# Weights through GpSimd's queue in the load stage, a comparison in two parts, and the last X W products between own half rows

## The chip, the cores and the metric

The kernel runs on one core of one Trainium2 chip. The metric is the device time of one execution in microseconds (us). Three timed executions of the kernel before gave 1069.7, 1071.4 and 1076.45 us, with the median 1071.4 us.

## The reference, cut to what matters

Four graph layers with a residual and a layer norm behind each work on N = 2708 nodes with 128 features and a 2708 x 2708 adjacency matrix in float32.

```
x = norm(x + L0(x, adj));  x = norm(x + L1(x, adj));  x = norm(x + L2(x, adj));  x = norm(x + L3(x, adj))

L0: d = 1/sqrt(adj.sum(-1));  z = leaky_relu((d * (adj @ (d * x))) @ W1 + b1, 0.1)
    S = exp(-dist(z_i, z_j) / 2), only the 4 largest of a row kept
    A2 = S + adj;  d2 = 1/sqrt(A2.sum(-1));  out = (d2 * (A2 @ (d2 * x))) @ W2 + b2
L1: XW = X @ W;  c = XW @ a[:128];  r = XW @ a[128:]
    den = exp(leaky_relu(r[:, None] + c[None, :], 0.01));  num = A @ den
    att = where(num != 0, den / num, 0);  H = A @ (att @ XW)
L2: d = 1/sqrt(adj.sum(1) + 1e-6);  (d * (adj @ (d * x))) @ W.T + b
L3: relu(concat([x, adj @ x]) @ W.T + b)
```

In L1 the kernel sorts the nodes by c, so that the two branches of the leaky relu become sums over the nodes on either side of an edge in that order. For this it needs the rank of every node's c among all c.

## The kernel before, in words

The matrix is passed in transposed. It is cut into 22 row tiles of 128 rows (the last one has 20) and into six column chunks with 512, 512, 512, 512, 384 and 276 columns. Row tiles 0 to 15 are streamed in panels of four tiles; tiles 16 to 21 stay in the resident tile `res`, filled chunk by chunk.

**Load stage** (lines 461 to 520). A loop over the chunks c = 0 to 5 issues, all on SyncE's queue (SP): the rows of x (`load_x`, L132), three panels into a pool of four `part` buffers and the fourth panel into a slot of `ring` (`load_panel`, L178), the resident tiles (L472) and the last 20 rows (L477). VectorE adds all panels into `both` (L479, L483, L484), which gives the degrees of the chunk's nodes; TensorE sums `both` over the partitions (L496); VectorE and ScalarE make `dinv` and the scaled rows `y` of this chunk (L501, L242, L243, L260). TensorE also adds the products of the panels with the y that is known already (`add_group`, L428): in step c the groups g = 0 to c - 1, with the group of chunk c - 1's own panel put in after the first. At c = 4 the eleven loads of weights and biases (`load_const` and `load_rows`, L143) stand behind chunk 4's panels on SP's queue and ahead of chunk 5's. The biases and the attention vector are read as one row repeated for 128 partitions. `ring` and `res` are zeroed first by GpSimd (L125, L120), and a panel that goes into `ring` waits for that. In this stage only TensorE's order is written out by hand; the order of the other engines is a planner's. Behind the loop TensorE adds what is left (`rest`, `add_few`), and the next stage computes all distances for the four nearest neighbours.

**Pass 2 of L0** (`by_panels` with `end_pass2`, L993). Here the order of TensorE, VectorE and ScalarE is the program's. `by_panels` calls a tick after every product, and `end_pass2` places the work on a finished chunk at ticks counted from n: `norm0` (L800, L805), `turn` (transposes L818, copied by ScalarE L821), `find_c` (a product L872 gives the chunk's c for all partitions, copied into `c_row` by ScalarE L873; VectorE L877 takes each node's own c), then for each tile t `compare` (VectorE: a mask of c_row >= c_t, L904, and ties, L914), `times_w` (X W, L885, L886), `rank_rows` (ScalarE sums the mask's rows, L922) and `rank_columns` (TensorE sums its columns, L927). The last chunk (tiles 19 to 21) is done otherwise: `last_stats`, `last_rc` (c and r of the three tiles, L847, L850), `turn_c` (transposes L866, copied into `c_row` by ScalarE L867), then the comparisons of tiles 19 and 20 and `compare_few`. In `find_ranks` (L949) everything is joined.

**Lists of L1** (lines 1104 to 1505). A table `turns` writes out the order: `line` adds one half row tile of the matrix that was streamed into a berth (L1387, 8 matmul records, and the load of the line that follows in this berth, L1062), `own_line` one from `res`, and between them stand the steps that build the sorted lists. `last_xw` forms X W for tiles 19 to 21: a transpose (L1180), ScalarE's copy (L1182), the product (L1184), ScalarE's copy (L1186) and GpSimd's store (L1187), tile after tile. `in_rank_order` and `in_list_order` (L1228) put values into order by one-hot matrices `hot_in` (L1218), `counts` (L1314, L1321) counts list lengths, `ranked` and `listed` write down the indices with which GpSimd gathers rows.

The block stage of L1 and the layers 2 and 3 come behind that. Their text is not touched.

Of the kernel before, what the change touches and what calls it, by code (L numbers as in the profile page):

```python
# [8 lines left out]
F32 = mybir.dt.float32  # L9
U32 = mybir.dt.uint32  # L10
I32 = mybir.dt.int32
BF16 = mybir.dt.bfloat16
# [4 lines left out]
P = 128  # L17
CW = 512
RES = 6
# [33 lines left out]
def kernel(  # L53
# [42 lines left out]
    def few(c):  # L96
        g = c % GROUPS * 32
        return slice(g, g + LAST)
# [41 lines left out]

    def load_const(src, cols, name):
        t = const.tile([P, cols], F32, tag=name, name=name)
        nc.sync.dma_start(t, src)  # L143
        return t

    def load_rows(src, cols, name):
# [217 lines left out]
    with tc.tile_pool(name="knn", bufs=1) as knn:  # L364
# [97 lines left out]
        with (  # L462
# [5 lines left out]
            for c in range(C):  # L468
                w = cw[c]
                load_x(chunk_tiles[c])  # L470
                parts = [load_panel(g, c, load if g < G - 1 else None) for g in range(G)]
                nc.sync.dma_start(  # L472
                    res[:, : FULL - S, cols[c]],
                    adjT[S * P : FULL * P, cols[c]].rearrange("(t p) k -> p t k", p=P),
                )
                if LAST:
                    nc.sync.dma_start(res[few(c), FULL - S, cols[c]], adjT[FULL * P :, cols[c]])  # L477
                both = degp.tile([P, 2, CW], F32, tag="both", name="both")
                nc.vector.tensor_add(both[:, :, :w], parts[0][:, :2, :w], parts[0][:, 2:, :w])  # L479
                more = [part[:, n : n + 2, :w] for part in parts[1:] for n in (0, 2)]  # L480
                more += [res[:, n : n + 2, cols[c]] for n in range(0, RES, 2)]
                for m in more:
                    nc.vector.tensor_add(both[:, :, :w], both[:, :, :w], m)  # L483
                nc.vector.tensor_add(both[:, 0, :w], both[:, 0, :w], both[:, 1, :w])  # L484

                for g in range(min(c, G)):
                    add_group(c, g, parts[g])
                    if wait is not None:
                        add_group(*wait)
                        wait = None  # L490
                if c == C - 1:
                    add_group(c, G, None)
                ts = chunk_tiles[c]
                dps = mis_tile()
                for k, t in enumerate(ts):
                    nc.tensor.matmul(  # L496
                        dps[: pw[t], k : k + 1], lhsT=both[:, 0, k * P : k * P + pw[t]], rhs=ones, start=True, stop=True
                    )
                full = sum(pw[t] == P for t in ts)
                t0, t1 = ts[0], ts[-1] + 1  # L500
                nc.vector.tensor_copy(deg[:, t0 : t0 + full], dps[:, :full])  # L501
                if t0 + full < t1:
                    nc.vector.tensor_copy(deg[:LAST, t0 + full : t1], dps[:LAST, full : full + 1])
                inv_sqrt(dinv[:, t0:t1], deg[:, t0:t1])
                scale_rows(y, xs, dinv, ts)
                if c == C - 1:
                    spread(y[:, FULL, :])
                wait = (c, c, parts[c] if c < G else None, c == C - 1)
                if c == C - 2:
                    w1_sb = load_const(w1, D, "w1")  # L510
                    w2_sb = load_const(w2, D, "w2")
                    wa_sb = load_const(w_att, D, "w_att")
                    wl_sb = load_const(w_lap_t, D, "w_lap")
                    wx_sb = load_const(w_cat_t[:D, :], D, "w_cat_x")
                    wh_sb = load_const(w_cat_t[D:, :], D, "w_cat_h")
                    b1_sb = load_rows(b1, D, "b1")
                    b2_sb = load_rows(b2, D, "b2")
                    bl_sb = load_rows(b_lap, D, "b_lap")
                    bc_sb = load_rows(b_cat, D, "b_cat")
                    a_sb = load_rows(a_att, 2 * D, "a_att")  # L520


            def rest(c, g, end=False):
# [316 lines left out]
            nc.vector.bn_aggr(mv[: pw[t], t, :], st[: pw[t]])  # L840
        inv_sqrt_of(rstd_l, mv[:, l0:l1, 1], LN_EPS, True)

    def last_rc():

        both = rc_of(C - 1, lambda t: P)
        for v, dst in ((1, cc), (0, rr)):
            nc.vector.scalar_tensor_tensor(  # L847
                dst[:, l0:l1], mv[:, l0:l1, 0], w_sum[:, v : v + 1], both[:, v, :], op0=ALU.mult, op1=ALU.subtract
            )
            nc.vector.scalar_tensor_tensor(  # L850
                dst[:, l0:l1], dst[:, l0:l1], -1.0, rstd_l, op0=ALU.mult, op1=ALU.mult
            )

    def last_norm():
        for t in last_ts:
# [40 lines left out]

    split = {T - 2: (T - 1) * P // 2}

    def compare(t):
        p, o = pw[t], t * P  # L900
        s = cc[:p, t : t + 1]
        mask = masks[t] = sum_pool.tile([P, N], BF16, tag="mask", name="mask", bufs=4)
        m = split.get(t, o + p)
        nc.vector.tensor_scalar(mask[:p, :m], c_row[:p, :m], s, None, op0=ALU.is_ge)  # L904
# [84 lines left out]

    ended = [-16]  # L990
    behind_last = []

    def end_pass2(c, acc):  # L993
        n = max(due.n + 1, near_at[chunk_tiles[c][-1]] + 3, ended[-1] + 16)
# [8 lines left out]
        if c < C - 1:  # L1003
            at(n + 2, norm0, ts)
            at(n + 9, turn, c)
            at(n + 11, find_c, c)
            for k, t in enumerate(ts):
                at(n + 13 + 2 * k, compare, t)
                at(n + 14 + 2 * k, times_w, c, t)
# [94 lines left out]
    with tc.tile_pool(name="rank", bufs=1) as rank:  # L1104
# [67 lines left out]
        c_part = pick_c(edge, "first")  # L1172
        last_norm()

        def last_xw():

            for t in last_ts:
                p = pw[t]
                pt = mis_tile()
                nc.tensor.transpose(pt[:, :p], xs[:p, t, :], ident[:p, :p])  # L1180
                xT = small.tile([P, P], F32, tag="z", name="xT")
                nc.scalar.copy(xT[:, :p], pt[:, :p])  # L1182
                po = mis_tile()
                nc.tensor.matmul(po[:p, :D], lhsT=xT[:, :p], rhs=wa_sb, start=True, stop=True)  # L1184
                row = small.tile([P, P], F32, tag="junk", name="row")
                nc.scalar.copy(row[:p], po[:p, :D])  # L1186
                nc.gpsimd.dma_start(xw_rows[t * P : t * P + p, :], row[:p])  # L1187

        def whole(dst, src, n):

# [283 lines left out]
        def own_line(n):  # L1474
# [373 lines left out]
```

## Time and profile before

| | us |
|---|---|
| median of three timed executions | 1071.4 |
| profiled execution, its own time | 1068.27 |
| its span in the profile | 1066.5 |
| load stage, until the last degree sum of TensorE | 0 to 105.6 |
| rest of the first pass and the neighbour search | 105.6 to 300 |
| pass 2 until the last mask product (L942) | 300 to 448.4 |
| lists of L1 | 448.4 to 507 |
| block stage of L1 | 507 to 731 |
| last tiles of L1, layers 2 and 3 | 731 to 1066.5 |

The profile shows one execution. PE is TensorE's matmul, PEld its weight load, DVE VectorE, ACT ScalarE, POOL GpSimd, SP SyncE; SPq is SP's queue. In a timeline a row gives the start, the time taken, the engine, the line, the operation, the tiles (out<-in), the shape, the count and, in brackets, the idle time before it with what ended it. In a table of windows each row is a stretch: its length, then for PE, PEld, DVE, ACT and POOL the busy time and the number of instructions, then the clock granted to TensorE as a share of full speed, the DMA engines' busy share and GB/s.

### The profile page before, as it was taken

How to read it: one execution, taken by the hardware profiler on the slowest of the kernel's cores; microseconds unless marked ns; L12 is line 12 of the kernel's file. 1: busy time of each engine (PE TensorE's matmuls, PEld its weight loads, DVE VectorE, ACT ScalarE, POOL GpSimd, SP SyncE). 2: the span in 40 equal slices, each digit the busy share in tenths (PEclk: the TensorE clock that was granted, in tenths of full speed). 3: DMA queues.
4: the chain of work that ended last, by engine and by line, in shares of the span. 5: the costliest groups of instructions: out<-in, count | busy, mean ns of one | idle time of the engine just before them, and what ended most of it. 6: DMA issues, size and time to landing. Idle time of an engine off the chain costs nothing.

```text
span 1066.5 us, 11660 instructions
## 1 busy us (share of the span) xinstructions
PE 983.9 (92%) x3773; PEld 481.8 (45%) x3773; DVE 637.6 (60%) x1363; ACT 331.9 (31%) x609; POOL 264.9 (25%) x339
## 2 busy tenths in 40 slices
PE   0888999999994998799899999999999999999996
PEld 0346544444442556654333333334445544564444
DVE  5985438999943578674798999995121121222222
ACT  0000126555500244612776776663010100010000
POOL 4000000000564565005766443430121100000000
PEclk9989999999997999699999999999999999999998
DMA  9998350000183666587565455456755856484652
GB/s 338 363 340 268 114 160 1 0 1 1 42 278 113 202 184 209 199 357 260 144 172 150 137 141 165 133 169 202 232 189 173 292 181 216 145 276 145 229 166 74
DMA packets 102001, 191.00 MB, mean 179 GB/s; under 512 B 14022, under 2 KB 43342, under 8 KB 101930
## 3 DMA queue, kind: packets, MB, share of 16 engines
q1 hardware_dynamic: 83896, 152.34, 43.1%
q0 software_dynamic: 17728, 37.62, 12.8%
q8 instruction: 32, 0.52, 0.2%
q14 instruction: 39, 0.32, 0.1%
q10 hardware_dynamic: 306, 0.20, 0.1%
HBM read 214.80 MB, written 4.16 MB: 205 GB/s over the span
## 4 chain that ended last, share of the span: by engine, by line
PE 48%; DVE 1%; ACT 1%; issue 0%; DMA 0%; POOL 0%; SPq 0%; POOLq 0%
PE acc L204 27%; PE hacc L1536 10%; PE num L1654 9%; PE mis L285 1%; PE mis L1783 0%; DMA ring<-carry 0%; ACT gb L234 0%; PE mis L1749 0%; DVE inv L1525 0%; PE mis L1779 0%; DVE inv L1528 0%; ACT inv L1511 0%; POOL rstd L253 0%; DVE err L1521 0%; PE mis L1737 0%
## 5 line engine op out<-in xcount | busy, mean ns | idle before, releaser
L1095 POOL DMA_INDIRECT ring<-in_adjT,slot_i x88 | 96.6, 1098 | 93.8 <-PE num L1654 72.1
L1654 PE MATMUL num<-ring,lw 128*64 128x512 f32 (+1 forms) x528 | 111.9, 550 | 4.0 <-DVE err L1521 1.9
L1536 PE MATMUL hacc<-inv,xws 128*128 128x512 f32 (+1 forms) x264 | 111.7, 559 | 1.7 <-ACT xws L1699 1.4
L705 PE MATMUL acc<-zT,z 128*128 128x512 f32 (+2 forms) x252 | 102.2, 552 | 0.0
L1511 ACT ACTIVATE inv<-num,plain 128x1024 f32<-128x1024 f32 x88 | 80.5, 915 | 59.3 <-PE num L1654 38.9
L253 POOL TENSOR_TENSOR rstd<-rstd,minus_half 128x4 f32<-128x4 f32 (+1 forms) x18 | 17.3, 959 | 313.5 <-DVE rstd L252 313.5
L234 ACT COPY gb<-acc 128x512 f32<-128x512 f32 (+2 forms) x18 | 9.6, 534 | 251.1 <-PE acc L204 251.1
L706 ACT COPY key<-acc 128x512 f32<-128x512 f32 (+2 forms) x126 | 67.1, 534 | 55.1 <-PE acc L705 27.7
L204 PE MATMUL acc<-ring,y 128*128 128x512 f32 (+2 forms) x192 | 83.3, 564 | 0.5 <-issue 0.5
L750 POOL DMA_INDIRECT got<-y_rows,where x66 | 70.8, 1073 | 45.8 <-DVE near_sum L763 25.9
L1536 PEld LDWEIGHTS hacc<-inv,xws 128*128 128x128 f32 x264 | 46.5, 189 | 78.7 <-issue 53.4
L1521 DVE TENSOR_TENSOR err<-inv,num 128x1024 f32<-128x1024 f32 x88 | 73.8, 852 | 10.2 <-DMA carry<-m_rows 4.9
L204 PE MATMUL acc<-ring,xs 128*128 128x512 f32 (+2 forms) x192 | 77.6, 547 | 0.0
L1528 DVE SCALAR_TENSOR_TENSOR inv<-gb,g_inv,inv 128x1024 f32<-128x1024 f32 x88 | 77.0, 912 | 0.1
L204 PE MATMUL acc<-ring,carry 128*128 128x512 f32 (+2 forms) x192 | 74.5, 542 | 0.0
L204 PE MATMUL acc<-ring,m_rows 128*128 128x512 f32 (+2 forms) x192 | 74.3, 542 | 0.0
L1525 DVE SCALAR_TENSOR_TENSOR inv<-err,inv 128x1024 f32<-128x1024 f32 x88 | 72.2, 858 | 0.1
L705 PEld LDWEIGHTS acc<-zT,z 128*128 128x128 f32 x252 | 45.8, 190 | 50.4 <-issue 45.0
L1514 ACT ACTIVATE inv<-inv 128x1024 f32<-128x1024 f32 x88 | 67.6, 768 | 2.8
L575 POOL TENSOR_TENSOR slot_e<-near,sim 128x44 f32<-128x44 f32 (+2 forms) x3 | 0.7, 238 | 259.3 <-DVE near L572 259.2
L709 DVE MAX8 near<-key 128x8 f32<-128x2708 f32 x21 | 62.3, 2965 | 2.6 <-ACT key L706 2.6
L1654 PEld LDWEIGHTS num<-ring,lw 128*64 128x64 f32 x528 | 35.6, 136 | 62.4 <-issue 44.6
(378 smaller groups left out, 1368.9 us busy)
## 6 DMA issues: line engine op xcount, KB each, us to landing
ring<-in_adjT SPq DMA_DIRECT2D x74, 1024.0 KB
ring<-in_adjT SPq DMA_DIRECT2D x20, 677.0 KB
ring<-in_adjT SPq DMA_DIRECT2D x17, 768.0 KB
part<-in_adjT SPq DMA_DIRECT2D x12, 1024.0 KB
ring<-in_adjT SPq DMA_DIRECT2D x17, 552.0 KB
more<-in_adjT SPq DMA_DIRECT2D x10, 677.0 KB
res<-in_adjT SPq DMA_DIRECT2D x4, 1280.0 KB
part<-in_adjT SPq DMA_DIRECT2D x3, 768.0 KB
```

What stands on the lines that cost most here:

```text
L204: nc.tensor.matmul(accs[c][: lhsT.shape[-1], :w], lhsT=lhsT, rhs=src, start=start, stop=stop)
L705: nc.tensor.matmul(pks[c][:p, : cw[c]], lhsT=z2[:, :p], rhs=zT[:, cs], start=False, stop=True)
L706: nc.scalar.copy(key[:p, cs], pks[c][:p, : cw[c]])
L750: nc.gpsimd.indirect_dma_start(out=got[:p, :], out_offset=None, in_=y2_rows[:, :], in_offset=bass.IndirectOffsetOnAxis(ap=where[:p, t, k : ...
L1095: nc.gpsimd.indirect_dma_start(out=rows[i][:KC, n, :], out_offset=None, in_=adj_half[:, :], in_offset=bass.IndirectOffsetOnAxis(ap=slot_i[ ...
L1511: nc.scalar.activation(inv, num[:, :w], AF.Ln, scale=plain[:, 0:1], bias=plain[:, 1:2])
L1514: nc.scalar.activation(inv, inv, AF.Exp, scale=-1.0)
L1521: nc.vector.tensor_mul(err, inv, num[:, :w])
L1525: nc.vector.scalar_tensor_tensor(inv, err, 2.0, inv, op0=ALU.subtract, op1=ALU.mult)
L1528: nc.vector.scalar_tensor_tensor(inv, gb[:, col : col + w], g_inv[:, q : q + 1], inv, op0=ALU.max, op1=ALU.mult)
L1536: nc.tensor.matmul(haccs[:, o:e], lhsT=xws[:, q, :], rhs=inv[:, o:e], start=(q == 0), stop=(q == NQ - 1))
L1654: nc.tensor.matmul(num[n * (BJ + 2) : (n + 1) * (BJ + 2), o:e], lhsT=lw[:, 2 * q + n, :], rhs=rows[i][:, n, c0 + o : c0 + e], start=True, ...
```

## The change

There are five edits.

1. `load_const` issues on GpSimd's queue instead of SP's, and the eleven weight loads stand at c = 1, ahead of that chunk's panels in the program, instead of at the end of c = 4.
2. In chunk 0 the panel that goes into `ring` is issued behind the resident tiles and the last rows, and VectorE adds it last. Chunks 1 to 5 keep their order.
3. The row sum of the mask of tile 15 (the last tile of the fourth chunk) moves on ScalarE behind `turn` and `find_c` of the fifth chunk: `behind_turn`.
4. In the last chunk `last_rc` is split: c of the three tiles comes first, then `turn_c`, then the part of tile 19's mask that needs the columns below 2432 only (`compare_known`), then the rest of it in `compare`; r of the three tiles and its negative come two ticks later, ahead of tile 20's comparison.
5. `last_xw` is split into `turn_last` and `last_xw(t)`, and one line or own half row stands between the two for each of the tiles 19, 20 and 21. Two own lines are taken for that from the group of four ahead of `ranks_known`.

```
     def load_const(src, cols, name):
         t = const.tile([P, cols], F32, tag=name, name=name)
-        nc.sync.dma_start(t, src)
+        nc.gpsimd.dma_start(t, src)
...
                 load_x(chunk_tiles[c])
-                parts = [load_panel(g, c, load if g < G - 1 else None) for g in range(G)]
+                if c == 1:
+                    w1_sb = load_const(w1, D, "w1")
...
+                    a_sb = load_rows(a_att, 2 * D, "a_att")
+                parts = [load_panel(g, c, load) for g in range(G - 1)]
+                if c:
+                    parts.append(load_panel(G - 1, c))
                 nc.sync.dma_start(
                     res[:, : FULL - S, cols[c]],
...
                     nc.sync.dma_start(res[few(c), FULL - S, cols[c]], adjT[FULL * P :, cols[c]])
+                if not c:
+                    parts.append(load_panel(G - 1, c))
...
-                more += [res[:, n : n + 2, cols[c]] for n in range(0, RES, 2)]
+                held = [res[:, n : n + 2, cols[c]] for n in range(0, RES, 2)]
+                more = more + held if c else more[:-2] + held + more[-2:]
...
-                if c == C - 2:
-                    w1_sb = load_const(w1, D, "w1")
...
-                    a_sb = load_rows(a_att, 2 * D, "a_att")
...
-    def last_rc():
-
-        both = rc_of(C - 1, lambda t: P)
-        for v, dst in ((1, cc), (0, rr)):
...
+    def last_of(v, dst):
+
+        if not unscaled:
+            unscaled.append(rc_of(C - 1, lambda t: P))
...
+    def compare_known(t):
+        masks[t] = sum_pool.tile([P, N], BF16, tag="mask", name="mask", bufs=4)
+        nc.vector.tensor_scalar(
+            masks[t][:, : l0 * P], c_row[:, : l0 * P], cc[:, t : t + 1], None, op0=ALU.is_ge
+        )
...
+            if c == C - 2:
+                for t in behind_turn:
+                    at(n + 11, rank_rows, t)
...
+                elif c == C - 3 and k == len(ts) - 1:
+                    behind_turn.append(t)
...
-            at(n + 3, last_rc)
+            at(n + 3, last_of, 1, cc)
             at(n + 3, turn_c, c)
-            at(n + 3, negate_r)
+            at(n + 3, compare_known, ts[0])
+            at(n + 5, last_of, 0, rr)
+            at(n + 5, negate_r)
...
-            (line, 4), (blocks_of_edges,), (line, 7), (last_xw,), (in_rank_order, 0), (line, 3),
+            (line, 4), (blocks_of_edges,), (line, 6), (turn_last, T - 3), (line, 1), (last_xw, T - 3),
+            (turn_last, T - 2), (own_line, 1), (last_xw, T - 2), (turn_last, T - 1), (own_line, 1), (last_xw, T - 1),
+            (in_rank_order, 0), (line, 3),
             (in_rank_order, 1), (line, 3), (in_rank_order, 2), (count_lone,), (line, 2), (counts,), (line, 3),
-            (add_last_rows, 0), (own_line, 4), (ranks_known,), (line, 2), (own_line, 1), (in_list_order, 0),
+            (add_last_rows, 0), (own_line, 2), (ranks_known,), (line, 2), (own_line, 1), (in_list_order, 0),
```

More of the change, by code (lines that the diff above doesn't have):

```diff
@@ L470 @@
                 load_x(chunk_tiles[c])
-                parts = [load_panel(g, c, load if g < G - 1 else None) for g in range(G)]
+                if c == 1:
+                    w1_sb = load_const(w1, D, "w1")
+                    w2_sb = load_const(w2, D, "w2")
+                    wa_sb = load_const(w_att, D, "w_att")
+                    wl_sb = load_const(w_lap_t, D, "w_lap")
+                    wx_sb = load_const(w_cat_t[:D, :], D, "w_cat_x")
+                    wh_sb = load_const(w_cat_t[D:, :], D, "w_cat_h")
+                    b1_sb = load_rows(b1, D, "b1")
+                    b2_sb = load_rows(b2, D, "b2")
+                    bl_sb = load_rows(b_lap, D, "b_lap")
+                    bc_sb = load_rows(b_cat, D, "b_cat")
+                    a_sb = load_rows(a_att, 2 * D, "a_att")
+                parts = [load_panel(g, c, load) for g in range(G - 1)]
+                if c:
+                    parts.append(load_panel(G - 1, c))
                 nc.sync.dma_start(
@@ L508 @@
                 wait = (c, c, parts[c] if c < G else None, c == C - 1)
-                if c == C - 2:
-                    w1_sb = load_const(w1, D, "w1")
[L511 to L519, printed above, removed]
-                    a_sb = load_rows(a_att, 2 * D, "a_att")
             def rest(c, g, end=False):
@@ L841, in last_stats @@
         inv_sqrt_of(rstd_l, mv[:, l0:l1, 1], LN_EPS, True)
-    def last_rc():
-        both = rc_of(C - 1, lambda t: P)
-        for v, dst in ((1, cc), (0, rr)):
[L847 to L852, printed above, removed]
+    unscaled = []
+    def last_of(v, dst):
+        if not unscaled:
+            unscaled.append(rc_of(C - 1, lambda t: P))
+        nc.vector.scalar_tensor_tensor(
+            dst[:, l0:l1], mv[:, l0:l1, 0], w_sum[:, v : v + 1], unscaled[0][:, v, :], op0=ALU.mult, op1=ALU.subtract
+        )
+        nc.vector.scalar_tensor_tensor(
+            dst[:, l0:l1], dst[:, l0:l1], -1.0, rstd_l, op0=ALU.mult, op1=ALU.mult
+        )
     def last_norm():
@@ L897 @@
     split = {T - 2: (T - 1) * P // 2}
+    def compare_known(t):
+        masks[t] = sum_pool.tile([P, N], BF16, tag="mask", name="mask", bufs=4)
+        nc.vector.tensor_scalar(
+            masks[t][:, : l0 * P], c_row[:, : l0 * P], cc[:, t : t + 1], None, op0=ALU.is_ge
+        )
     def compare(t):
@@ L901, in compare @@
         s = cc[:p, t : t + 1]
-        mask = masks[t] = sum_pool.tile([P, N], BF16, tag="mask", name="mask", bufs=4)
+        e = l0 * P if t in masks else 0
+        if not e:
+            masks[t] = sum_pool.tile([P, N], BF16, tag="mask", name="mask", bufs=4)
+        mask = masks[t]
         m = split.get(t, o + p)
-        nc.vector.tensor_scalar(mask[:p, :m], c_row[:p, :m], s, None, op0=ALU.is_ge)
+        nc.vector.tensor_scalar(mask[:p, e:m], c_row[:p, e:m], s, None, op0=ALU.is_ge)
         if m < o + p:
@@ L991 @@
     behind_last = []
+    behind_turn = []
     def end_pass2(c, acc):
@@ L1173, with turn_last, last_xw @@
         last_norm()
[L1175 to L1187, printed above, removed]
+        last_rows = {}
+        def turn_last(t):
+            p = pw[t]
+            pt = mis_tile()
+            nc.tensor.transpose(pt[:, :p], xs[:p, t, :], ident[:p, :p])
+            xT = last_rows[t] = small.tile([P, P], F32, tag="z", name="xT")
+            nc.scalar.copy(xT[:, :p], pt[:, :p])
+        def last_xw(t):
+            p = pw[t]
+            po = mis_tile()
+            nc.tensor.matmul(po[:p, :D], lhsT=last_rows[t][:, :p], rhs=wa_sb, start=True, stop=True)
+            row = small.tile([P, P], F32, tag="junk", name="row")
+            nc.scalar.copy(row[:p], po[:p, :D])
+            nc.gpsimd.dma_start(xw_rows[t * P : t * P + p, :], row[:p])
         def whole(dst, src, n):
```

## The prediction, written before the changed kernel ran

> **What bounds the kernel now.** I read the page first: TensorE is busy for 92% of the span. The chain that ended last covers only the time from 517 us on, so for the three places of the change I read table of windows and timeline there.
>
> ```profile
> PE 983.9 (92%) x3773; PEld 481.8 (45%) x3773; DVE 637.6 (60%) x1363; ACT 331.9 (31%) x609; POOL 264.9 (25%) x339
> ```
>
> Place one is the end of the load stage. First SP's queue, then TensorE's timeline, then windows:
>
> ```profile
> 73.22 0.84 SPq L143 DMA_DIRECT2D w<-in_w x2
> 82.39 0.43 SPq L143 DMA_DIRECT2D a_att<-in_a_att x1
> 83.85 2.98 SPq L178 DMA_DIRECT2D part<-in_adjT x3
> ```
> ```profile
> 92.44 3.25 PE L428 MATMUL acc<-part,y 128*128 128x276 f32 x8 [3.01 <-DMA part<-in_adjT]
> 98.03 3.88 PE L428 MATMUL acc<-part,y 128*128 128x276 f32 x16
> 105.00 0.64 PE L496 MATMUL mis<-ones,both 128*128 128x1 f32 x6
> ```
> ```profile
> 84.00:86.00 2.00, 2.00 (x8) 1.19 (x7) 1.75 (x4) 0.00 (x0) 0.00 (x0) 1.00 0.12 26
> 94.00:96.00 2.00, 2.00 (x5) 1.33 (x4) 1.92 (x3) 0.00 (x0) 0.00 (x0) 0.50 1.11 332
> ```
>
> The weights hold SP from 73.2 to 82.8 us, and from 81 to 88 us the DMA engines move about 43 GB/s of single repeated rows, where panels move 385. So chunk 5's panels land late, TensorE stands for 3.01 us, and then its clock is half for about 3 us.
>
> Place two is the fifth chunk in pass 2 (ScalarE's timeline, then TensorE's) and the end of that pass (VectorE's):
>
> ```profile
> 422.84 1.92 ACT L922 ACTIVATE junk<-mask 128x2048 bf16<-128x2048 bf16 x1
> 424.65 0.20 ACT L922 ACTIVATION_READ_ACCUMULATOR junk<-mask 128x1 f32 x1
> 424.74 0.47 ACT L821 COPY xT<-mis 128x384 f32<-128x384 f32 x1
> ```
> ```profile
> 425.27 1.65 PE L872 MATMUL mis<-xT,w_c 128*128 128x384 f32 x2 [2.65 <-ACT xT L821]
> 426.71 2.96 PE L204 MATMUL acc<-ring,y 128*128 128x276 f32 x6
> ```
> ```profile
> 442.59 1.55 DVE L904 TENSOR_SCALAR mask<-hT,cc 128x2560 bf16<-128x2560 f32 x1 [0.82 <-ACT hT L867]
> ```
>
> The transposes ended at 420.6, but the copy stands behind a mask sum of 2.1 us that nobody needs yet. Place three is `last_xw`, in TensorE's timeline:
>
> ```profile
> 462.22 0.49 PE L1184 MATMUL mis<-w_att,xT 128*128 128x128 f32 x2 [0.35 <-ACT xT L1182]
> 463.24 0.49 PE L1184 MATMUL mis<-w_att,xT 128*128 128x128 f32 x2 [0.41 <-ACT xT L1182]
> 464.16 0.40 PE L1184 MATMUL mis<-w_att,xT 128*20 128x128 f32 x2 [0.27 <-ACT xT L1182]
> ...
> 466.45 3.03 PE L1387 MATMUL acc<-ring,lc 128*32 128x339 f32 x24
> ...
> 470.87 1.91 PE L1387 MATMUL acc<-ring,lc 128*32 128x339 f32 x24
> ```
>
> Three waits, and behind them the same 24 records cost 3.03 us at half clock and 1.91 at full.
>
> [...]
>
> **The change part by part**, against the profiled execution (1068.27 us; 3.1 us under the median of the timed ones, so I add 3.1 at the end).
>
> Edit 1, removed: with no weights ahead of them chunk 5's panels are issued as `part` buffers come free: the first at about 74 (TensorE's group (3,2) ends), the second at 77.7, the third at 83.6 (group (4,1)); ring and resident tiles follow by 85. DMA is done with chunk 4 by about 80, so the first lands long before 89.4, when TensorE wants it, and the others by 91. TensorE then runs on. Its work from 92.44 to 105.00 took 12.56 us; at full clock it is four groups of 8 at 1.94 (half of 3.88), 2.05 for six of 384 columns (8 took 2.74) and 1.46 for six of 276: 11.27. Gain 3.0 + 1.3 = 4.3 us. Next in line is the degree sum of chunk 5: VectorE ends chunk 4 at 85.8 and needs 8 us for chunk 5, so by about 94 to 95, and TensorE asks at 100.7. From 100 us on TensorE is busy in every window to 150, then VectorE is full through the search, which begins with TensorE's last zT; so this gain is carried on.
>
> Edit 1, added: eleven issues on GpSimd. Its stores at L1187 take 0.57 us each with gaps of 0.3 us, so about 10 us between 13.7 (its last zeroing) and 24, where it has nothing else until 272. The bytes, 768 KB, are 2.0 us at 385 GB/s in chunks 0 to 2, and there DMA does decide: VectorE's sum of chunk 2 waited at 51.63 for the resident tiles (0.93 us), and TensorE's work runs on from that sum (56.25) without a gap to 89.4. Against it stand two DMA dips: 0.75 us at 10 to 14 and 1.36 us at 32 to 36. The first goes with edit 2 (SP no longer stands at 10.04 for the zeroing), the second is filled by the weights. So +2.0 - 2.1 = 0 at best. The repeated rows cost more: bounded by 0 and by the 7 us that they took alone. I take +0.4[...].
>
> Edit 2: the order of chunk 0 removes VectorE's waits of 1.45 and 0.32 us. That is hidden, since chunk 2's DMA ends last; counted at nothing beyond the dip.
>
> Edit 3: the copy L821 starts at 422.84 instead of 424.74, so L872 is 1.9 us earlier. ScalarE does the sum behind find_c's copy, where it stood for 2.71 us; so it delays nobody, and the mask's buffer is wanted next by tile 19 only. If the shorter gap (0.40 + 0.75 us remain) does not drop the clock, more is won: 425.27 to 431.70 took 6.43 us, and its rows at full speed (0.86 + 1.40 + 0.22 + 0.93 + 0.22) take 3.6. Then ScalarE's copies and mask sums limit: one after the other they reach the copy of the last chunk (L1000) at about 431.6 instead of 436.22, 4.5 us. Between 1.9 and 4.5 I take 3.2.
>
> Edit 4: from L904's rows 0.52 ns an element and 0.22 us fixed; 2432 columns 1.48 us, 128 columns 0.28. From 441.15: 1.48 + 0.28 less 0.08 overlap, ties 0.27, r 0.45, its negative 0.2, so tile 20 starts at 443.75 instead of 444.33. 0.6 us won: 0.82 of waiting less 0.21 for splitting. Row sums and e_r on ScalarE are ready before, and L942 follows VectorE.
>
> Edit 5: 1.03 us of waits filled by two own lines (0.62 each) and a line, which are wanted later anyway. If the clock stays up, 464.48 to 469.41 (4.93 us) becomes the 3.30 of the rows behind it: another 1.6. So 1.0 to 2.6; I take 2.4, as nothing idle is left. VectorE's one-hot tiles were ready at 463.7, TensorE arrives at about 464.5 minus the other gains, all of which move both. Behind `counts` VectorE needs 3.3 us and TensorE still has 3.9 us of lines, so removing two own lines there opens no wait.
>
> Sum: -4.3 + 0.4 - 3.2 - 0.6 - 2.4 = -10.1. Profiled 1058.2; with 3.1 the forecast is 1061.
>
> **The rivals.**
> - The clock falls anyway in places two and three: -4.3 + 0.4 - 1.9 - 0.6 - 1.0 = -7.4, so 1064. For it: small waits were enough at 464. Against it: waits of 0.96 us at 495 to 497 left the clock at full.
> - The repeated rows keep their 7 us in the stream of panels: less 2.1 us of dips, +4.9 at chunk 2, so -10.5 + 4.9 = -5.6, 1066. For it: at 81 to 88 they had the DMA engines nearly alone and were slow. Against it: the DMA engines' busy share there was only 0.1 to 0.5.
> - Slower: all 768 KB go at that 43 GB/s and panels wait as long, 18 us in chunks 1 and 2, less 2.1: +15.9 - 10.5 = +5.4, 1077. It decides from 12.6 us of lost panel time on. Against it: the six plain weights passed at 344 to 406 GB/s together with panels.
>
> Two holds that the profile calls remote could also move[...]: ScalarE at L1000 (until 336.10, about 12 us behind TensorE's result) and VectorE at L1344 (until 497.00, 2.5 us). The first lies ahead of every changed instruction of ScalarE; I leave both where they are, with 3 us either way in the range.
>
> **How the numbers follow.** Forecast 0.50, clock 0.22, repeated rows 0.20, slower 0.08. The range 1054 to 1070 holds the first three with their unknowns: -4.5 for edit 3, -2.6 for edit 5 and 3 for the holds below, the rows' case and 4 above. One per cent, about what a measurement of this kernel tells from no change, is 10.7 us, so below 1060.7 counts as faster. That is about half of the forecast's own cases and a part of the others: 0.36. Slower by over 1% 0.07, the rest 0.57.
>
> **What would show it.** In the new profile: no TensorE wait for `part` near 89 and full clock there; y of chunk 2 within 1 us of 57.95; L872 0.8 us behind L204 instead of 2.65; tile 20's mask 0.6 us earlier relative to cc; no waits at L1184. A DMA share near 1 with low GB/s at 15 to 35 us, or TensorE's start on chunk 2's y later by over 5 us, would prove me wrong.

## The result and the profile after

The changed kernel takes 1063.17 us (median of 6 runs, 1059.73 to 1065.55) where the kernel before, run beside it, takes 1074.27 us: ratio 0.9897, 95% interval 0.9871 to 0.9923, so 11.1 us or 1.0% less. The forecast was 1061 with a range of 1054 to 1070; it started from 1071.4, the median of the first three executions of the kernel before, where all six give 1074.27. Two later comparisons of the same two kernels gave 0.9877 (0.9848 to 0.9906) and 0.9901 (0.9865 to 0.9937).

The pair of profiled executions alone would have misled: 1065.55 us after (span 1063.8) against 1068.27 us before (span 1066.5), only 2.7 us. Where the other 8 us are is worked out further down.

The page's first line, for the engines, has hardly moved; a change of one per cent doesn't show there:

```profile
PE 982.1 (92%) x3773; PEld 479.4 (45%) x3773; DVE 637.3 (60%) x1364; ACT 331.5 (31%) x609; POOL 273.5 (26%) x350
```

**The load stage.** TensorE's timeline, first chunk 1's degree sum in the kernel before, then the changed kernel (start, length, line, operation, and in brackets the idle time ahead of it and what ended it):

```profile
40.07 1.05 PE L496 MATMUL mis<-ones,both 128*128 128x1 f32 x8 [2.98 <-DVE both L484]
```
```profile
43.64 1.87 PE L513 MATMUL mis<-ones,both 128*128 128x1 f32 x8 [6.65 <-DVE both L501]
...
60.61 13.98 PE L428 MATMUL acc<-part,y 128*128 128x512 f32 x32
...
90.71 2.11 PE L428 MATMUL acc<-part,y 128*128 128x276 f32 x8
...
102.01 0.64 PE L513 MATMUL mis<-ones,both 128*128 128x1 f32 x6
```

At the end of the stage things are as foreseen: no wait for `part` (3.01 us before), and the row of 8 takes 2.11 us instead of 3.25. The last degree sum is at 102.01 instead of 105.00. But at its start there is something that the prediction did not have: TensorE waits 6.65 us for chunk 1's sum, which comes at 43.64 instead of 40.07, and y of chunk 2 is used from 60.61 on instead of 57.95. VectorE of the changed kernel and one window, of the kernel before and then of the changed one, show what happens there:

```profile
30.09 2.49 DVE L500 TENSOR_TENSOR both<-both,part 128x1024 f32<-128x1024 f32 x2 [2.71 <-DMA part<-in_adjT]
```
```profile
core 0: us, PE busy (x) PEld busy (x) DVE busy (x) ACT busy (x) POOL busy (x), PEclk, DMA share, GB/s
24.00:26.00 2.00, 1.87 (x8) 1.78 (x8) 0.04 (x2) 0.00 (x0) 0.00 (x0) 1.00 1.05 388
24.00:26.00 2.00, 1.23 (x6) 1.14 (x6) 0.73 (x2) 0.20 (x1) 0.00 (x0) 1.00 0.99 150
```

VectorE stands 2.71 us for a panel. Between 24 and 26 us the DMA engines are occupied for 0.99 of the time and move 150 GB/s; in the kernel before it was 388. On either side of this window the changed kernel moves 313 and 344.

**The fifth chunk in pass 2, and the last one.** TensorE's timeline, then VectorE's:

```profile
425.43 0.91 PE L879 MATMUL mis<-xT,w_c 128*128 128x384 f32 x2 [0.75 <-ACT xT L826]
426.18 1.56 PE L204 MATMUL acc<-ring,y 128*128 128x276 f32 x6
```
```profile
438.52 1.49 DVE L908 TENSOR_SCALAR mask<-hT,cc 128x2432 bf16<-128x2432 f32 x1
439.96 0.29 DVE L920 TENSOR_SCALAR mask<-hT,cc 128x128 bf16<-128x128 f32 x1
```

The wait at the product of `find_c` is 0.75 us instead of 2.65, and the clock stays up. The six records of 276 columns behind it take 1.56 us instead of 2.96. The windows show the same (of the kernel before, then of the changed one); PEclk is the third number from the right:

```profile
429.00:431.00 2.00, 2.00 (x7) 1.62 (x6) 2.00 (x5) 0.86 (x2) 0.00 (x0) 0.50 0.26 38
```
```profile
429.00:431.00 2.00, 2.00 (x25) 1.70 (x25) 2.00 (x6) 2.00 (x3) 0.00 (x0) 1.00 0.87 302
```

The numbers of records, 7 and 25, don't compare, since 16 of the 25 are short sums of a mask's columns. The landmarks do: from the product of `find_c` to the last chunk's first `norm0` product it takes 8.48 us (425.43 to 433.91) instead of 11.39 (425.27 to 436.66).

**The lists.** The waits at the products of `last_xw` are gone, and the 24 records that took 3.03 us at half clock take 1.91:

```profile
460.02 0.49 PE L1213 MATMUL mis<-w_att,xT 128*128 128x128 f32 x2
...
461.20 0.38 PE L1213 MATMUL mis<-w_att,xT 128*20 128x128 f32 x2
...
462.98 1.91 PE L1416 MATMUL acc<-ring,lc 128*32 128x339 f32 x24
```

So every part does something like what it was meant to do. Summed along the landmarks of this pair of profiles the parts give 3.0 + 4.8 + 0.7 + 2.3 = 10.8 us. The profile's own difference is smaller because in this one execution ScalarE is held longer than before in two places, in pass 2 behind chunk 1 and at the end of the lists, by more than it is held shorter behind chunk 0. A hold means here that an engine starts an instruction well after its operands are written; where the profile says "remote", it names no instruction of this core as what ended the wait.

### The profile page after: what moved, and what is told of

Same layout as the page of the kernel before. It is cut to its first block, busy times and chain, and to the rows that moved or that the text cites. A ratio compares the mean times of both kernels' runs of the same rounds, so it can differ in the third digit from the quotient of the medians.

```text
span 1063.8 us, 11669 instructions
## 1 busy us (share of the span) xinstructions
PE 982.1 (92%) x3773; PEld 479.4 (45%) x3773; DVE 637.3 (60%) x1364; ACT 331.5 (31%) x609; POOL 273.5 (26%) x350
## 4 chain that ended last, share of the span: by engine, by line
PE 49%; DVE 1%; ACT 1%; issue 0%; DMA 0%; POOL 0%; POOLq 0%
PE acc L204 28%; PE hacc L1567 10%; PE num L1685 9%; PE mis L285 1%; PE mis L1814 0%; DMA ring<-carry 0%; ACT gb L234 0%; PE mis L1780 0%; DVE inv L1556 0%; PE mis L1810 0%; DVE inv L1559 0%; ACT inv L1542 0%; POOL rstd L253 0%; DVE err L1552 0%; ACT inv L1545 0%
## 5 line engine op out<-in xcount | busy, mean ns | idle before, releaser
L710 PE MATMUL acc<-zT,z 128*128 128x512 f32 (+2 forms) x252 | 102.2, 552 | 0.0
L1542 ACT ACTIVATE inv<-num,plain 128x1024 f32<-128x1024 f32 x88 | 80.5, 914 | 60.5 <-PE num L1685 51.8
```

The lines of the kernel that those rows point to most:

```text
L710: nc.tensor.matmul(pks[c][:p, : cw[c]], lhsT=z2[:, :p], rhs=zT[:, cs], start=False, stop=True)
L1542: nc.scalar.activation(inv, num[:, :w], AF.Ln, scale=plain[:, 0:1], bias=plain[:, 1:2])
```

## The experiments

There are twelve runs of nine kernels, in three groups of four. Every ratio is to the kernel before, run in the same group. In the second group everything, the kernel before too, took some 20 us less; the third group, on the same chip, took again what the first had taken on another. Times are therefore compared within a group only.

| kernel | median us | before us | ratio | 95% interval |
|---|---|---|---|---|
| load_only | 1072.65 | 1072.93 | 0.9996 | 0.9970 to 1.0023 |
| pass2_only | 1067.88 | 1072.93 | 0.9948 | 0.9925 to 0.9971 |
| lists_only | 1067.32 | 1072.93 | 0.9954 | 0.9936 to 0.9972 |
| weights_last | 1060.71 | 1072.93 | 0.9876 | 0.9832 to 0.9920 |
| after_again | 1041.33 | 1053.88 | 0.9877 | 0.9848 to 0.9906 |
| weights_sp_early | 1047.86 | 1053.88 | 0.9937 | 0.9913 to 0.9961 |
| weights_last_again | 1036.72 | 1053.88 | 0.9860 | 0.9819 to 0.9901 |
| pool_dmas | 1053.31 | 1053.88 | 0.9997 | 0.9979 to 1.0014 |
| after_more | 1064.03 | 1074.13 | 0.9901 | 0.9865 to 0.9937 |
| weights_last_more | 1059.92 | 1074.13 | 0.9871 | 0.9833 to 0.9908 |
| old_chunk0 | 1059.96 | 1074.13 | 0.9867 | 0.9823 to 0.9910 |
| rows_last | 1060.89 | 1074.13 | 0.9877 | 0.9841 to 0.9914 |

Theory: the parts add up, each with the size that its stage shows. Rival: the 11 us came from the holds of ScalarE, which the profile calls remote and which differ from execution to execution. The first three kernels do one stage's part alone.

**load_only**: the hunks of the load stage, nothing else.

```
-        nc.sync.dma_start(t, src)
+        nc.gpsimd.dma_start(t, src)
...
+                if c == 1:
+                    w1_sb = load_const(w1, D, "w1")
...
+                more = more + held if c else more[:-2] + held + more[-2:]
```

> The kernel before with the load stage's part of the change alone (weights on GpSimd's queue ahead of chunk 1, new order of loads in chunk 0). Theory 1, the parts add up: 3 to 4 us faster than before (TensorE's wait of 3.0 us and the half clock behind it near 90 us go, chunk 1's late degree sum is paid out of slack), ratio about 0.997. Theory 2, the time was won by shorter holds[...]: no relation to the 3 us; anything between +4 and -8 us, while the last degree sum of the load stage in the profile still ends 3 us earlier. Theory 3, the repeated rows of the biases cost chunk 1 what the end of the stage gains: within 1 us of before. In the profile the degree sum of chunk 1 is at about 43.6 us instead of 40.1 in all three.

Measured: 0.4 us faster by the ratio, interval 3.2 faster to 2.5 slower. In its profile chunk 1's degree sum is at 43.77 and the stage ends at 102.30, both as expected. So about 2 us are won at 105 us, and they are hardly to be seen at the end. Theory 1's 3 to 4 us lie at the edge of the interval or beyond it; 2 us can't be told from theory 3.

**pass2_only**: the hunks of pass 2.

```
+            if c == C - 2:
+                for t in behind_turn:
+                    at(n + 11, rank_rows, t)
...
+            at(n + 3, last_of, 1, cc)
             at(n + 3, turn_c, c)
+            at(n + 3, compare_known, ts[0])
+            at(n + 5, last_of, 0, rr)
```

> The kernel before with the two parts in pass 2 alone (tile 15's mask sum behind the turn of the fifth chunk's row of c; the last chunk's cc ahead of its rr, with the known columns compared first). Theory 1: 5.4 us faster (4.7 at the fifth chunk, of which 1.8 is the wait and 2.9 the clock that stays up, and 0.7 at the last), ratio about 0.995; in the profile the third product behind find_c runs at full clock. Rival, only the wait counts and the clock falls all the same: 2.5 us. Theory 2, holds: no relation to 5.4.

Measured: 5.6 us faster by the ratio (0.52%; interval 3.1 to 8.0), against 5.4 expected. The wait is 0.76 us, the clock 1.00 throughout 426 to 432. From the product of `find_c` to the first product of gb it takes 19.55 us, as in the changed kernel (19.54); with the old text it was 23.17 (before), 23.12 (load_only) and 23.18 (pool_dmas). The rival with 2.5 us is out.

**lists_only**: the new table of turns and the divided `last_xw`.

```
-            (line, 4), (blocks_of_edges,), (line, 7), (last_xw,), (in_rank_order, 0), (line, 3),
+            (line, 4), (blocks_of_edges,), (line, 6), (turn_last, T - 3), (line, 1), (last_xw, T - 3),
+            (turn_last, T - 2), (own_line, 1), (last_xw, T - 2), (turn_last, T - 1), (own_line, 1), (last_xw, T - 1),
+            (in_rank_order, 0), (line, 3),
```

> The kernel before with the list stage's part alone (turns and products of the last rows apart, with own lines between). Theory 1: 2.3 us faster, 1.0 from the waits and 1.3 from the clock, ratio about 0.998, and the three waits at last_xw's products are gone. Rival, the clock falls all the same: 1.0 us. Theory 2, holds: no relation to 2.3.

Measured: 4.9 us faster by the ratio (interval 3.0 to 6.9), twice what was expected. The three alone add up to 0.4 + 5.6 + 4.9 = 10.9 us, where the whole gave 11.1, 10.6 and 13.0: they add up, within intervals of 2 to 3 us for each, but not with the sizes of the first pair of profiles. Why the lists are worth more is to be seen in the kernels that still have the old order there. The windows of the kernel before:

```profile
464.00:466.00 2.00, 1.84 (x13) 1.64 (x13) 1.90 (x5) 0.36 (x3) 1.11 (x2) 0.83 1.02 420
466.00:468.00 2.00, 2.00 (x15) 0.95 (x18) 1.97 (x6) 0.00 (x0) 0.00 (x0) 0.50 1.01 412
468.00:470.00 2.00, 2.00 (x22) 0.93 (x14) 1.90 (x9) 0.00 (x0) 0.00 (x0) 0.81 1.03 408
470.00:472.00 2.00, 2.00 (x25) 1.36 (x28) 2.00 (x2) 0.00 (x0) 0.00 (x0) 1.00 1.01 412
```

and of pass2_only, whose list stage has the same text and begins 2 us earlier:

```profile
462.00:464.00 2.00, 1.93 (x12) 1.73 (x13) 1.92 (x4) 0.27 (x2) 1.12 (x2) 0.75 1.03 422
464.00:466.00 2.00, 2.00 (x16) 1.10 (x19) 1.94 (x5) 0.00 (x0) 0.00 (x0) 0.50 1.01 413
466.00:468.00 2.00, 2.00 (x16) 0.38 (x8) 1.90 (x10) 0.00 (x0) 0.00 (x0) 0.50 1.03 404
468.00:470.00 2.00, 2.00 (x13) 1.86 (x9) 2.00 (x4) 0.00 (x0) 0.00 (x0) 0.50 1.01 414
470.00:472.00 2.00, 2.00 (x14) 1.17 (x17) 1.36 (x2) 0.00 (x0) 0.00 (x0) 0.50 1.02 420
472.00:474.00 2.00, 2.00 (x22) 0.70 (x14) 0.00 (x0) 0.00 (x0) 0.00 (x0) 0.69 1.01 406
```

In windows of 0.5 us the clock of the kernel before is 1.00 until 465, 0.84 in the next, 0.50 from 465.5 to 468.5, then 0.75 and 1.00 again. I take it to be either full or half; then a window of 2 us at a mean clock of 0.83 was at half for (1 - 0.83) x 2 x 2 = 0.7 us. By this estimate the half clock lasts 3.4 us in the kernel before and in pool_dmas, and 10.2 us in pass2_only and load_only, behind the same waits (0.35, 0.41 and 0.27 us). TensorE is busy all through both. At half clock the six records of 276 columns took 2.96 us and at full clock 1.56 (above), so I estimate the cost of a half clock as half its length, and the waits with what they bring along as 1.0 + 1.7 = 2.7 us or 1.0 + 5.1 = 6.1 us. The measured 4.9 lies between. The stage as a whole, from the first product of gb to the block stage, takes 55.8 us in lists_only, 59.1 in the kernel before and 62.1 in pass2_only, which fits. Each length is seen in one profile each of two kernels; which of them the timed executions of the kernel before have is not known. In lists_only and in the changed kernel the clock is 1.00 from 456 to 486 us.

**weights_last**: the changed kernel with the eleven loads on SP's queue, behind chunk 5's panels.

```
-        nc.gpsimd.dma_start(t, src)
+        nc.sync.dma_start(t, src)
...
-                if c == 1:
...
                 if LAST:
                     nc.sync.dma_start(res[few(c), FULL - S, cols[c]], adjT[FULL * P :, cols[c]])
+                if c == C - 1:
+                    w1_sb = load_const(w1, D, "w1")
```

> The changed kernel, but the eleven weight loads go out on SyncE's queue behind all of chunk 5's panels, where nobody waits for a panel any more (the weights themselves are first wanted at about 110 us). Theory 1: chunk 1's degree sum comes at 40 us or earlier again instead of 43.6, no wait for chunk 5's panels either, and if TensorE has no spare time between chunk 2 and chunk 5 this is carried to the end: 2 to 4 us faster than the changed kernel, 1060. Rival: DMA decides the stage as a whole and chunk 2's loads end last whatever the order of the weights; then only the 2.0 us of the weights' bytes come back, less the DMA dips that they filled, 0 to 1 us. Slower: the weights' repeated rows hold up the ring's first panels of the work behind chunk 5, over 1 us slower than the changed kernel, with a wait for ring near 115 us.

Measured: 1060.71 us, 1.2% under the kernel before. Chunk 1's sum is back at 39.85, chunk 5's panels are not waited for, and the stage ends at 100.02. TensorE has no wait at all between 98 and 160 us, so nothing waits for the weights or for `ring` either. The changed kernel is not in this group, so how much faster than it this is stays open here; the later groups have both.

The first group left a question: why load_only keeps so little of its 2 us. The profiles up to then differ in one more thing, ScalarE's copy of the last lines:

```profile
506.91 0.44 ACT L1407 COPY m_rows<-acc 128x338 f32<-128x338 f32 x1 [3.18 <-PE acc L1387]
```
```profile
503.46 0.44 ACT L1436 COPY m_rows<-acc 128x338 f32<-128x338 f32 x1 [3.85 <-remote]
```
```profile
513.09 0.44 ACT L1412 COPY m_rows<-acc 128x338 f32<-128x338 f32 x1 [4.55 <-remote]
```

These are the kernel before, the changed kernel and load_only. Where the weights are on GpSimd, the copy is held, and TensorE stands 2.5 us instead of 0.7 ahead of the block stage; in pass2_only, lists_only and weights_last it is not held. Theory H (H for hold): the loads on GpSimd set this off, and so eat the load stage's gain. The second group tests it.

**after_again**: the changed kernel.

> The changed kernel as it is, for a second profile and more timed runs beside the others of this call. Theory H (the weights on GpSimd's queue set off a hold of ScalarE at the end of the list stage, which eats what the load stage gains): its copy of the last lines (m_rows) waits 3 to 5 us in a wait that the profile calls remote, as in the two profiles so far that have the weights on GpSimd, and the block stage begins 2 to 3.5 us late. Rival, the holds come by chance: no such wait this time, or another length. The half clock behind the third of last_xw's products is gone in both. Time 1062, ratio 0.990.

Measured: 1041.33 us, ratio 0.9877. No hold at `m_rows`, and none anywhere else:

```profile
482.17 0.44 ACT L1436 COPY m_rows<-acc 128x338 f32<-128x338 f32 x1 [3.17 <-PE acc L1416]
```

So the hold doesn't follow from the loads on GpSimd alone. But none of the four profiles of this group has any remote wait between 230 and 530 us, so the rival isn't shown by it either: what holds ScalarE was absent as a whole.

**weights_sp_early**: the changed kernel, loads at the same place ahead of chunk 1, on SP's queue.

```
-        nc.gpsimd.dma_start(t, src)
+        nc.sync.dma_start(t, src)
```

> The changed kernel with the weights at the same place ahead of chunk 1, but on SyncE's queue. SyncE's chunk 1 panels are issued some 4.5 us later, so the degree sum of chunk 1 comes at 44 to 48 us and the load stage ends at 102 to 105 us. Theory H: no remote wait at m_rows, so 2 to 3 us come back there: time within 1.5 us of the changed kernel or up to 3 us below it. Rival, chance: remote waits as in the changed kernel, and 0 to 3 us slower than it through the load stage.

Measured: 1047.86 us, 6.5 us over after_again, more than either theory expected. Chunk 1's sum is at 46.38 (after_again 43.63) and the stage ends at 105.97 (101.69), later than with the old place. At this place GpSimd's queue is worth 4.3 us of the load stage: SP's eleven issues stand ahead of its own panels. On SP's queue the rows were slow in the kernel before too: 35 GB/s from 81 to 88 us. The rest of the 6.5 us is not explained, and the ranges overlap (1042.6 to 1050.5 and 1037.8 to 1046.6).

**weights_last_again**: the same kernel as weights_last.

> The kernel with the weights on SyncE's queue behind chunk 5's panels once more, now beside the changed kernel. The load stage ends at 100.0 us (2.0 below the changed kernel). Theory H: no remote wait at m_rows either, so 4 to 5 us faster than the changed kernel, 1057.5, ratio to before 0.986. Rival, chance: 2 us faster than the changed kernel.

Measured: 1036.72 us, 4.6 us below after_again; the stage ends at 99.19, 2.5 us earlier, and the first z behind the stage follows exactly (108.16 against 110.67). The ranges of the two overlap (1032.8 to 1046.4 and 1037.8 to 1046.6), so 4.6 isn't told from 2.5.

**pool_dmas**: the kernel before, with eleven loads of 8 bytes a partition on GpSimd's queue.

```
+                if c == 1:
+                    spare = const.tile([P, 22], F32, tag="spare", name="spare")
+                    for n in range(11):
+                        nc.gpsimd.dma_start(spare[:, 2 * n : 2 * n + 2], x[:P, 2 * n : 2 * n + 2])
```

> The kernel before, with eleven loads of 8 bytes for each of 128 partitions added on GpSimd's queue at about 13 us, into a tile that nobody reads; the weights stay where they were. The load stage may lose up to 3 us[...] and ends at 105 to 108 us. Theory H: the remote wait of 3 to 5 us at m_rows appears, and the kernel is 2 to 3 us slower than before on top of what the load stage loses. Rival, chance: no such wait, slower by what the load stage loses alone.

Measured: ratio 0.9997 (0.9979 to 1.0014), the stage ends at 104.91. Eleven more loads on GpSimd as such cost nothing. On the hold it says nothing, because this group had none.

Having no holds, this profile and after_again's are also the cleanest pair, since pool_dmas is the kernel before but for eleven loads that cost nothing. Between the two the load stage differs by 3.2 us, pass 2 by 5.5 (1.9 between the `find_c` products of chunks 0 and 4, 3.6 from there to the first product of gb) and the lists by 2.4: 11.1 us, the size of the gain. Outside the parts 1.2 us more are won ahead of chunk 0's `find_c` and 1.9 lost behind the lists, neither of them explained; the spans are 1053.0 and 1042.6. The rival of the first group, that the gain came from the holds, is out with this: the gain is there without any.

**after_more**: the changed kernel, third group.

> The changed kernel once more, as the base for the other three of this call: load stage's last degree sum at 101.7 to 102.0 us, chunk 1's at 43.6 us; ratio to before 0.988 to 0.990.

Measured: 1064.03 us, ratio 0.9901. Chunk 1's sum at 43.84, the stage ends at 102.86. The hold at `m_rows` is back, with the length of the first time:

```profile
504.42 0.44 ACT L1436 COPY m_rows<-acc 128x338 f32<-128x338 f32 x1 [3.83 <-remote]
```

Outside the second group it is there in all three profiles that have the eleven loads on GpSimd (3.83 to 4.55 us) and in none of the six that have them on SP (before, pass2_only, lists_only, weights_last, weights_last_more, old_chunk0). rows_last, with six of them on GpSimd, lies between: no remote wait is named, but TensorE stands 2.0 us for the copy, where it stood 0.7 in those six. That speaks for theory H where there are holds at all, and 1.9 us of TensorE's time hang on it, about what load_only lost; a mechanism is not shown.

**weights_last_more**: the same kernel as weights_last.

> The weights on SyncE's queue behind chunk 5's panels, for more timed runs beside the changed kernel: 2 to 5 us faster than it (2.0 and 2.5 us of the load stage in two pairs of profiles, 4.6 us between the medians of the last call). Rival: within 1 us, because the rest of the run eats it.

Measured: 1059.92 us, 4.1 us below after_more. Its stage:

```profile
39.35 1.37 PE L513 MATMUL mis<-ones,both 128*128 128x1 f32 x8 [1.99 <-DVE both L501]
...
99.18 0.64 PE L513 MATMUL mis<-ones,both 128*128 128x1 f32 x6
```

**old_chunk0**: weights_last with the loads and sums of chunk 0 in the old order.

```
-                parts = [load_panel(g, c, load) for g in range(G - 1)]
-                if c:
-                    parts.append(load_panel(G - 1, c))
+                parts = [load_panel(g, c, load if g < G - 1 else None) for g in range(G)]
...
-                more = more + held if c else more[:-2] + held + more[-2:]
+                more += [res[:, n : n + 2, cols[c]] for n in range(0, RES, 2)]
```

> As the kernel with the weights behind chunk 5's panels, but with chunk 0's loads and sums in the order of the kernel before, so that of the load stage's change only the place of the weights is left. Theory of the prediction (the new order of chunk 0 is hidden): within 1 us of the kernel with the weights last, load stage at 99 to 100.5 us. Rival, the order of chunk 0 is part of the gain (SyncE no longer stands for the zeroing): chunk 1 and 2 come later and the load stage ends over 101 us.

Measured: 1059.96 us, the same as weights_last_more to 0.04 us; the stage ends at 99.69 against 99.18. So the new order of chunk 0 is worth half a microsecond of the stage at most, and nothing that the times show.

**rows_last**: the changed kernel with only the five repeated rows moved behind chunk 5's panels, on SP's queue.

```
-    def load_const(src, cols, name):
+    def load_const(src, cols, name, queue=None):
...
-        nc.gpsimd.dma_start(t, src)
+        (queue or nc.gpsimd).dma_start(t, src)
...
+        return load_const(bass.AP(...), cols, name, nc.sync)
...
-                    b1_sb = load_rows(b1, D, "b1")
...
+                if c == C - 1:
+                    b1_sb = load_rows(b1, D, "b1")
```

> The changed kernel with the six plain weights left on GpSimd's queue ahead of chunk 1 and the five loads that repeat one row in all 128 partitions moved to SyncE's queue behind chunk 5's panels. Theory, the repeated rows are what delays chunk 1: its degree sum comes at 40 to 41.5 us instead of 43.6 (only the 1.0 us of the 384 KB of plain weights is left), and the load stage ends within 1 us of the kernel with all weights last. Rival, the bytes or the six extra queue entries as such delay it: 42.5 us or later.

Measured: 1060.89 us, 3.1 us below after_more. TensorE's timeline, then the window that had 150 GB/s in the changed kernel:

```profile
40.13 1.86 PE L514 MATMUL mis<-ones,both 128*128 128x1 f32 x8 [2.56 <-DVE both L502]
...
99.36 0.64 PE L514 MATMUL mis<-ones,both 128*128 128x1 f32 x6
```
```profile
24.00:26.00 2.00, 1.52 (x8) 1.44 (x7) 0.44 (x2) 0.20 (x1) 0.00 (x0) 1.00 1.04 384
```

With the six plain weights still on GpSimd ahead of chunk 1, the sum is at 40.13, and the stage ends with that of weights_last_more. Where all weights are behind chunk 5, the sum comes at 39.35 to 39.85; so all but 0.3 to 0.8 us of chunk 1's delay comes from the five loads that read one row 128 times, 384 KB like the six others together.

The version to take is therefore one with the weights, or at least the rows, behind chunk 5's panels. Against the changed kernel of its group it is 3 to 5 us faster by medians in four comparisons (4.6, 4.1, 4.1, 3.1, the last three of them with the same six executions); no single pair of ratio intervals is apart, but the five profiles of such kernels end the load stage at 99.2 to 100.0 us and the four with all eleven on GpSimd at 101.7 to 102.9.

## Why the prediction was right, and which of its terms were not

The sum was -10.1 us and the result is -11.1 (by the ratios -10.6 and -13.0 in the repeats). The terms one by one:

- **Edit 1, removed (-4.3).** Right. From chunk 4's degree sum to chunk 5's it takes 11.88 us instead of 16.30, which is 4.4, with no wait for `part` and the clock at 1.00. Where nothing else pays for it, the last degree sum moves from 104.3 (mean of the four profiles with the old load stage) to 99.5 (mean of the five with the rows behind chunk 5): -4.8.
- **Edit 1, added (+0.4).** This is the term that was too small. The mean of the four with all weights on GpSimd is 102.2, so the weights at the new place cost 2.7 us. The prediction had named the repeated rows, bounded them by 0 and 7 us, and took 0.4; what spoke against more was the DMA engines' low share at 81 to 88 us. That did not hold: rows and panels together kept the DMA engines occupied at a share of 0.99 from 24 to 26 us while only 150 GB/s went through. So the low share in the kernel before, 0.25 from 81 to 88 us, was no sign that the rows leave room; why the share is low when they are alone, the runs don't show. (The windows give 35 GB/s there; the prediction's 43 is the mean from 80.5 us on, with the end of chunk 4's panels in it.) Of the 3.6 us that chunk 1 is late, 1.4 are left at the sum of chunk 3 (75.40 against 74.05), since y of chunk 2, 2.7 us late, is worked through in 13.98 us instead of 16.27: in the kernel before the clock is half from about 55.7 to 62.6 us, under this work, in the changed one from about 39.2 to 49.4, ahead of it and for 4.4 us in TensorE's wait. With the rows behind chunk 5, chunk 3's sum comes at 72.7 to 73.5. The rival with the repeated rows named the right loads and nearly double the size (+4.9). The announced sign, y of chunk 2 within 1 us of 57.95, failed, at 60.61; and "a DMA share near 1 with low GB/s", which by the prediction's words would prove it wrong, came true for one window of two microseconds. For this term it did.
- **Edit 2 (0).** Right within half a microsecond, by old_chunk0.
- **Edit 3 (-3.2, between -1.9 and -4.5).** The wait of 0.75 us is what was worked out (0.8), and the clock stayed up, so the upper end applied: -1.9 for the wait and -2.9 for the clock, -4.8. The middle between two cases that exclude each other was a value that neither would give.
- **Edit 4 (-0.6).** Right: 0.7, with 1.49 and 0.29 us for the two parts of tile 20's mask (1.48 and 0.28 forecast).
- **Edit 5 (-2.4).** Right where the old waits bring 3.4 us of half clock: 2.3 in the pair of profiles on which it was worked out, 2.4 between pool_dmas and after_again. Alone it gave 4.9. The half clock of 10.2 us behind the old waits in two other profiles is enough to explain that; that the timed executions have it is not shown. The term "another 1.6" for the clock was taken from one profile, and this quantity comes in two lengths, 3.4 and 10.2.
- **The rival "clock falls anyway"** did not come: neither at the fifth chunk nor behind `last_xw` does the changed kernel have the half clock of before (1.00 from 424 to 432 and from 456 to 486 us).
- **The rival "slower"** at 43 GB/s for all bytes did not come; the six plain weights cost chunk 1's sum less than a microsecond (40.13 against 39.35 to 39.85).

So the way was foreseen rightly, and that the total came out so close is luck: two errors cancel. The load stage is worth 2.1 us by the means of eight profiles, not 3.9, and where ScalarE's hold at `m_rows` comes, 1.9 of them seem to be lost again. Pass 2 and the lists, taken as 6.2, are worth 7.9 in the hold-free pair, since the half clock of the fifth chunk no longer happens and was counted only in part, and 10.5 in the two experiments.

The half clocks of the old waits last 3.4 and 10.2 us at the lists and, summed in the same way from 424 to 432 us, 6.8 us at the fifth chunk of the kernel before. What decides between these lengths is not shown: in pass2_only and load_only TensorE was busy throughout, and the clock was half for 10.2 us all the same. So the price of such a wait in this kernel is, by these profiles, that of 3.4 to 10.2 us at half clock.

**Where the 8 us between profiles and medians were.** ScalarE's copies at the end of chunks and lists are held past TensorE's result by an amount that differs between executions. In the first pair of profiles it goes like this. From the start of pass 2 to chunk 0's product of `find_c` the kernel before takes 59.94 us and the changed one 55.48: the hold here is shorter, and 4.5 us are won. From there to chunk 4's product it is 76.58 and 84.19, where edit 3 alone would give 74.7 (74.69 in after_again): 9.5 us are lost, 5.44 of them in TensorE's wait for ScalarE's copy of chunk 1, and behind it the clock is half (0.50 from 358 to 362 us). The lists take 59.06 and 59.08, where 2.3 less was due; 1.9 of that is the hold at `m_rows`. That makes 7.3 us, and 0.8 more come behind the lists. In the changed kernel, first group and second group:

```profile
327.67 0.58 ACT L1017 COPY hT<-acc 128x512 f32<-128x512 f32 x1 [30.17 <-remote]
```
```profile
321.46 0.59 ACT L1017 COPY hT<-acc 128x512 f32<-128x512 f32 x1 [24.26 <-PE acc L775]
```

The load stages of these two executions end 0.3 us apart (102.01 and 101.69), and the rows of y are written out within 0.3 us of each other (294.35 and 294.04). Then the product of `find_c` for chunk 0 starts at 341.24 and 333.69, the first product of gb at 444.97 and 427.92, the block stage at 504.05 and 482.76, and the spans are 1063.8 and 1042.6. The whole difference of 21 us arises between 294 and 504 us. The prediction left these holds where they were with 3 us either way. For the medians within a group that was enough; a pair of single profiles they moved by 7 us, and a whole group by 20, so a single profile pair was the wrong thing to subtract.

## What to carry to other kernels

When small loads are moved off a critical place, they have to go behind the last load that somebody waits for, not merely to another queue: ahead of chunk 1's panels, on GpSimd's queue, they made the load stage end at 102.2 us, behind chunk 5's panels at 99.5 (means of four and five profiles). Loads that repeat one row in all partitions cost far more here than plain ones of as many bytes (3.7 us of chunk 1's sum for 384 KB, where the six plain loads cost less than one). Waits on TensorE like the three here, 1.03 us in all, have to be priced with the half clock they may bring, and that price is read from several executions, since by the estimate above it was 1.7 us in some and 5.1 us in others. Subtract stage from stage between fixed landmarks before believing the difference of two spans.

## What the runs showed of the hardware that was not expected

- Loads that read one row for 128 partitions slowed other transfers beside them: 384 KB of them made chunk 1's sum 3.7 us late (43.84 us in after_more against 40.13 in rows_last), and from 24 to 26 us the DMA engines showed a busy share of 0.99 at 150 GB/s in the changed kernel, 1.04 at 384 GB/s in rows_last.
- The half clock behind three waits of 0.27 to 0.41 us lasted 3.4 us in two profiles (before, pool_dmas) and 10.2 us in two others (pass2_only, load_only), although TensorE was busy for 1.93 us or more of every 2 us in the long one that is shown.
- Waits of ScalarE and VectorE in the stages where GpSimd gathers rows (302 to 333 and 487 to 509 us in the kernel before) were prolonged in some executions: ScalarE's by 12.8 us in the kernel before (TensorE's result at 323.26, ScalarE's copy at 336.10) and by up to 14.9 us in weights_last_more (316.59 and 331.49), VectorE's by 2.6 us in the kernel before (494.41 and 497.00). In the four profiles of one group they were absent altogether, and every kernel of it took about 20 us less; in the changed kernel those 20 us lie in the stages with the holds. Why, and whether loads on GpSimd's queue move one of these holds to the end of the list stage, stays open.
